# First attention of a hybrid block on one core: another order of work within a group, ScalarE reading two more kinds of banks

## The chip, the cores and the metric

The kernel runs on one core of a Trainium2 chip. The core has five engines that run side by side, each with its own queue of instructions in a fixed order: TensorE (PE; its weight loads are listed as PEld), VectorE (DVE), ScalarE (ACT), GpSimd (POOL) and SyncE (SP, which only issues transfers here). An instruction that waits for another engine waits at the head of its queue, and everything behind it waits too. Products leave TensorE through PSUM, of which this kernel uses eight banks of 128 x 512 float32; ScalarE or VectorE must read a bank before it is given to another product.

The metric is the time of one execution in microseconds (us). Three runs of the kernel before took 2679.74, 2689.66 and 2694.45 us.

## The reference

The input is 16 sequences of 512 tokens with 256 features, all float32: 8192 tokens. Four layers follow each other, each with a residual sum:

```python
x = x + attn_a(layernorm(x))     # softmax attention, 16 heads of 16, rotary
x = x + ffn(layernorm(x))        # 64 routed experts, top 8, and a shared expert
x = x + attn_b(layernorm(x))     # linear attention with a forget gate
x = x + ffn(layernorm(x))

def attn_a(x):
    q, k, v = rope(proj(x, Wq)), rope(proj(x, Wk)), proj(x, Wv)
    attn = softmax(q @ k.T / 4)
    return (attn @ v) @ Wo.T

def ffn(x):
    probs = softmax(x @ router_w.T)
    w, ids = top_k(probs, 8); w = w / sum(w)
    ...
    gu = x @ ws_gate_up
    return routed + (silu(gu[:, :192]) * gu[:, 192:]) @ ws_down
```

The change lies in the first attention, with the part of the first `ffn` that needs no experts: its layernorm, the router and the shared expert.

## The kernel before, in words

A block is 512 tokens, one sequence; there are 16 blocks. Each block has four groups of four heads, and each group four steps, one for each 128 rows of keys or queries. A block is thus 16 steps, numbered 0 to 15 here; step 0 is the first step of group 0, step 4 of group 1, and so on. The order of all instructions of TensorE, VectorE, ScalarE and SyncE is written out by hand: `each(s)` yields the work of step `s`, and what is yielded first is issued first on every engine. GpSimd's order is left to the framework.

What every step does (function `each`, L451): `weighted` computes four score products of the current group `n` (L329, lhsT and rhs with 17 rows of the array for each head, the four heads side by side in the array), and ScalarE takes the exponential of each of the four banks (L369). `largest` computes four score products of group `n + 2` transposed (L329 with 16 rows), and VectorE takes the negated maximum of each bank (L343); the maxima later become a 17th row of the queries, so that the exponentials don't overflow.

What a group does once, with `n` its number:

- `summed(n - 1)` in its first step: 16 products of exponentials and values (L379) into one bank; ScalarE copies the bank (`heads_turned`, L144).
- `turn` of the keys of group `n + 3` in its first step, of the queries in its second: four transposes (L318) into one bank, copied by ScalarE (L323).
- `heads(n - 1)` in its second step (`heads_out`, L147): four transposes (L152) into one bank; VectorE takes the reciprocal of the sums (L156) and multiplies (L160), both reading the bank.
- `row(n + 1)` in its second step: one transpose of the maxima (L351), copied by ScalarE (L359), and four small transfers issued by SyncE that put it into the queries' 17th row.

What a block does once is in two tables, `dense` and `routed`, by step; `(work, far, ...)` means work for block `b + far`. The dense table loads and normalises the tokens two blocks ahead (`load`, `moments`, `normed`, `features`), projects queries and keys (`queries`, L255, with the rotation on GpSimd) and values (`values`, L299), and for the block behind joins the heads (`joined`, L225) and projects the output (`output`, L402; VectorE adds the bank to the residual, L409). The routed table does for the block behind the layernorm, transposes and router of the first `ffn` (`part.moments`, `normed`, `features` L1516, `logits` L1525, `likely`, `exps`), and for two blocks behind the choice of experts (`choose`), the counts (`count` L1582, `added` L1590 for three behind) and the shared expert (`shared`, with its products `gu` L1605 and its `silu` L991 to L993, and `down` L1636). Part of the shared expert of the last three blocks is done after the attention.

All products of this stage take their bank from one pool of eight, `bank()`, in program order and in rotation: the product that takes allocation number `k` waits until allocation `k - 8` has been read. A step takes eight banks for its scores, and one for each further product (`shared` with piece 0 takes two, `features` and `joined` two).

The functions that the diff touches are `heads_out`, `attention` with the inner `heads`, `output` and `each`, and the class `Part` of the `ffn` with `gu`, `silu` and `shared`.

Of the kernel before, what the change touches and what calls it, by code (L numbers as in the profile page):

```python
# [9 lines left out]
F32 = mybir.dt.float32  # L10
U32 = mybir.dt.uint32
AF = mybir.ActivationFunctionType
ALU = mybir.AluOpType
# [4 lines left out]
P = 128  # L18
D = 256
KD = D // P  # L20
H = 16
HD = D // H
HP = 32
NHG = 4
BLK = 512
# [12 lines left out]
class Block:  # L38
# [105 lines left out]
        self.nc.scalar.copy(oT, pav)  # L144
        return oT

    def heads_out(self, out, oT, hg, bank, den_eps=None):  # L147

        nc = self.nc
        pt = bank()  # L150
        for c in range(CB):
            nc.tensor.transpose(pt[:, ts(c, P)], oT[:, ts(c, P)], self.ident)  # L152
        o = pt.rearrange("p (c j k) -> p c j k", j=NHG, k=HP)
        rec = self.small.tile([P, CB, NHG], F32, name="rec")
        if den_eps is None:
            nc.vector.reciprocal(rec, o[:, :, :, HD])  # L156
        else:
            nc.vector.tensor_scalar(rec, o[:, :, :, HD], den_eps, None, ALU.add)
            nc.vector.reciprocal(rec, rec)
        nc.vector.tensor_tensor(  # L160
            out[:, :, ts(hg, NHG * HD)].rearrange("p c (j d) -> p c j d", d=HD),
            o[:, :, :, 0:HD],
            rec.unsqueeze(3).to_broadcast([P, CB, NHG, HD]),
            ALU.mult,
        )


    def attention(self, x, x1, wqkv, wo, rope, part, later):

# [9 lines left out]
        nc, tc = self.nc, self.tc  # L179
        with ExitStack() as c:  # L180
# [6 lines left out]
            p2 = c.enter_context(tc.tile_pool(name="a_2", bufs=2, side="left"))  # L187
# [200 lines left out]
            def heads(n):  # L388
                b, hg = divmod(n, NHG)
                if hg == 0:  # L390
                    aos[b] = p1.tile([P, CB, D], F32, name="ao")
                self.heads_out(aos[b], oTs.pop(n), hg, bank)


            def joined(b):
# [2 lines left out]
            def output(b, i):  # L398
                po = bank()
                for k in range(2):  # L400
                    for kd in range(KD):
                        nc.tensor.matmul(  # L402
                            po[:, ts(k, D)],
                            lhsT=aoTs[b][:, kd, ts(i + k, P)],
                            rhs=wo_sb[:, kd, :],
                            start=(kd == 0),
                            stop=(kd == KD - 1),
                        )
                nc.vector.tensor_tensor(  # L409
                    xs[b][:, i : i + 2, :],  # L410
                    xs[b][:, i : i + 2, :],
                    po.rearrange("p (c d) -> p c d", c=2),
                    ALU.add,
                )
# [6 lines left out]


            dense = {
                0: [(load, 2)],
                2: [(queries, 1, 2)],
                3: [(part.shared, -2, 1), (queries, 1, 3)],
                4: [(joined, -1)],
                6: [(values, 1, 0)],
                7: [(values, 1, 2)],
                8: [(moments, 2)],  # L430
                9: [(normed, 2)],
                10: [(output, -1, 0)],
                11: [(output, -1, 2)],
                13: [(features, 2)],
                14: [(queries, 2, 0)],
                15: [(queries, 2, 1)],
            }
            routed = {
                0: [(part.added, -3)],
                1: [(part.shared, -2, 0)],  # L440
                4: [(part.choose, -2, 0), (part.choose, -2, 1)],
                5: [(part.down, -2, 0), (part.choose, -2, 2)],
                9: [(part.down, -2, 2)],
                12: [(lambda b: part.moments(b, xs[b]), -1)],
                13: [(part.count, -2), (lambda b: part.normed(b, xs.pop(b)), -1)],
                14: [(part.features, -1)],
                15: [(part.logits, -1), (part.likely, -1), (part.exps, -1)],
            }
            steps, groups, z = NHG * CB, self.nblk * NHG, self.nblk - 1

            def each(s):  # L451

                n, i = divmod(s, CB)
                yield groups, n, weighted, i
                yield groups, n + 2, largest, i
                if i == 0:
                    yield groups, n - 1, summed
                    yield groups, n + 3, turn, kTs, H, "kT"
                if i == 1:
                    yield groups, n - 1, heads  # L460
                    yield groups, n + 1, row
                    yield groups, n + 3, turn, qTs, 0, "qT"
                b, at = divmod(s, steps)
                for work, far, *args in dense.get(at, []) + routed.get(at, []):

                    if b + far < z - 2 or work not in (part.shared, part.down):
                        yield self.nblk, b + far, work, *args

            with tc.manual_schedule(
                engines={  # L470
# [517 lines left out]
    def silu(self, out, gate, up, th, half):  # L988

        nc = self.nc  # L990
        nc.scalar.activation(th, gate, AF.Tanh, scale=0.5)  # L991
        nc.vector.scalar_tensor_tensor(th, th, 1.0, gate, ALU.add, ALU.mult)
        nc.vector.scalar_tensor_tensor(out, th, half, up, ALU.mult, ALU.mult)  # L993
# [380 lines left out]
class Part:  # L1374
# [6 lines left out]
    def __init__(self, ctx, k, x, y, weights, room, pairs, side):  # L1381
        rw, self.w_gate, self.w_up, self.w_down, ws_gu, ws_down = weights
        self.ctx, self.pairs, self.slot, self.ws = ctx, pairs, [], {}
        self.k, self.nc, self.x, self.y, self.room = k, k.nc, x, y, room
        tc, T = k.tc, k.T
        self.own = ctx.enter_context(ExitStack())
        self.pools = {
            n: self.own.enter_context(tc.tile_pool(name=f"r_{n}", bufs=n, side=side))
            for n in sorted({1, *room.values()})
        }  # L1390
        self.rows = k.dram.tile([T + P, ROW], F32, name="rows")
        self.counts = k.dram.tile([E, k.nch, P], F32, name="counts")
        (
            self.mvs,
            self.xns,
            self.xnTs,
            self.lgs,
            self.prs,
            self.tops,
            self.rests,  # L1400
            self.chosens,
            self.csums,
            self.hTs,
            self.ys,
            self.gus,
        ) = [{} for _ in range(12)]
        self.end = 0.0
        self.bank = None
        self.shared_weights = (rw, ws_gu, ws_down)
# [187 lines left out]


    def gu(self, b, piece):
        nc, xnT = self.nc, self.xnTs[b]  # L1600
        gu = self.gus[b, piece] = {}
        for m in ((0, 2), (1,))[piece]:
            gu[m] = self.bank()
            for kd in range(KD):
                nc.tensor.matmul(  # L1605
                    gu[m],
                    lhsT=self.wsg_sb[:, kd, ts(m, P)],
                    rhs=xnT[:, kd, :],
                    start=(kd == 0),
                    stop=(kd == KD - 1),  # L1610
                )
        if piece == 1:
            del self.xnTs[b]

    def silu(self, b, piece):
        if piece == 0:
            self.hTs[b] = self.hidden[b % len(self.hidden)]
        gu = self.gus.pop((b, piece))
        high = (P, FT)[piece]
        gate = gu[piece][0:high]  # L1620
        up = gu[2] if piece == 0 else gu[1][FT:P]
        th = self.tile("th", [P, BLK])[0:high]
        self.k.silu(self.hTs[b][0:high, piece, :], gate, up, th, 0.5)

    def shared(self, b, piece):
        self.gu(b, piece)
        self.silu(b, piece)
# [137 lines left out]
```

## Time and profile before

The profiled execution took 2689.83 us; its span, from the first to the last instruction, is 2688.0 us. The stages by time from the span's start, with the busy time of each engine:

| stretch, us | what runs | length | PE | DVE | ACT | POOL | clock |
|---|---|---|---|---|---|---|---|
| 62.20 to 224.46 | first attention, blocks 0 and 1 | 162.26 | 162.26 | 101.97 | 98.02 | 43.25 | 0.97 |
| 224.46 to 1227.69 | first attention, twelve full blocks | 1003.23 | 1003.23 | 695.44 | 599.18 | 235.79 | 1.00 |
| 1227.69 to 1372.70 | first attention, its last blocks | 145.01 | 144.78 | 82.97 | 82.11 | 15.33 | 0.91 |
| 1372.70 to 1700.00 | first experts | 327.30 | 251.62 | 194.72 | 94.56 | 188.97 | 0.90 |
| 1700.00 to 2160.00 | second attention | 460.00 | 442.79 | 438.31 | 262.83 | 119.95 | 1.00 |
| 2160.00 to 2688.00 | second experts | 528.00 | 400.81 | 343.11 | 143.67 | 223.29 | 0.89 |

The costliest rows of the twelve full blocks are the maxima (L343, 683 ns each on VectorE), the exponentials (L369, 602 ns each on ScalarE), the score products (L329) and the sums (L379).

How to read such a table: busy time says how much an engine did, not whether it set the pace. Matmuls are pipelined and a "busy" TensorE may be waiting between two records that overlap in the trace; the chain of waits, which goes back from the last instruction to what released it, and the timeline, which gives start and length of each run of instructions, tell that. The clock is the share of full TensorE clock that was granted.

### The profile page before, as it was taken

What the parts mean: (1) busy time and instruction counts of PE and PEld (TensorE: products, weight loads), DVE (VectorE), ACT (ScalarE), POOL (GpSimd) and SP (SyncE); (2) the same over time, 40 slices, a digit from 0 to 9 for tenths busy, and PEclk for the clock granted to TensorE, in tenths of its full rate; (3) what the DMA queues carried; (4) which work ended last, traced back from release to release, by engine and by line L of the source; (5) the groups of instructions that cost most, each with busy time, mean ns of one, the idle gap of its engine ahead of it and who ended that gap; (6) DMA issues with size and microseconds to landing.
All of it is one profiled execution on the core that took longest, in us unless ns stands there. A gap on an engine that the chain in (4) does not pass through costs nothing.

```text
span 2688.0 us, 47635 instructions
## 1 busy us (share of the span) xinstructions
PE 2447.6 (91%) x17864; PEld 1511.5 (56%) x17864; DVE 1895.4 (71%) x4646; ACT 1291.3 (48%) x2654; POOL 844.7 (31%) x804
## 2 busy tenths in 40 slices
PE   7999999999999999999988885899999969998781
PEld 3445455545455544555446775567667656667671
DVE  6666667666677666776646664899999869967650
ACT  1656556565566655665532332455555523323330
POOL 3122222122221222212015775332232122127773
PEclk7999999999999999999898998999999969999996
DMA  1000111001110001100158986201111058739987
GB/s 57 2 17 19 35 37 35 21 22 35 35 35 21 29 29 35 36 19 21 40 133 234 239 223 145 69 29 60 56 52 53 21 145 184 176 106 262 239 217 147
DMA packets 210003, 226.48 MB, mean 84 GB/s; under 512 B 34286, under 2 KB 202222, under 8 KB 208750
## 3 DMA queue, kind: packets, MB, share of 16 engines
q1 hardware_dynamic: 180366, 174.43, 22.5%
q0 software_dynamic: 25728, 46.15, 8.9%
q8 instruction: 143, 2.34, 0.4%
q10 hardware_dynamic: 3680, 2.85, 0.3%
q14 instruction: 86, 0.70, 0.1%
HBM read 146.50 MB, written 84.48 MB: 86 GB/s over the span
## 4 chain that ended last, share of the span: by engine, by line
PE 68%; DVE 15%; DMA 9%; issue 3%; POOL 1%; ACT 1%; SPq 0%; ACTq 0%; POOLq 0%; DVEq 0%
PE sc L329 20%; PE sc L379 9%; DMA xe<-rows,token 6%; PE sc L255 4%; DVE pT L841 4%; PE sc L1605 3%; PE sc L318 3%; DVE qkT L805 2%; PE sc L299 2%; PE sc L402 2%; PE sc L1636 2%; PE pb L792 2%; PE pb L717 2%; PE sc L1137 2%; PE sc L824 1%
## 5 line engine op out<-in xcount | busy, mean ns | idle before, releaser
L343 DVE TENSOR_REDUCE mx<-sc 128x1 f32<-128x512 f32 x1024 | 635.2, 682 | 375.7 <-PE sc L329 375.6
L369 ACT ACTIVATE pT<-sc 128x512 f32<-128x512 f32 x1024 | 528.6, 602 | 179.5 <-PE sc L329 179.5
L329 PE MATMUL sc<-qT,kT 17*128 17x512 f32 x2048 | 315.6, 646 | 0.0
L329 PE MATMUL sc<-kT,qT 16*128 16x512 f32 x2048 | 312.4, 609 | 1.5 <-DVE mx L343 1.4
L104 POOL TENSOR_SCALAR va<-mv 128x4 f32<-128x4 f32 x64 | 14.7, 230 | 797.1 <-DVE mv L98 797.1
L379 PE MATMUL sc<-pT,v 128*32 128x512 f32 x2048 | 241.8, 614 | 0.0
L329 PEld LDWEIGHTS sc<-kT,qT 16*128 16x128 f32 x2048 | 159.6, 189 | 94.4 <-issue 52.1
L841 DVE SCALAR_TENSOR_TENSOR pT<-sc,of,left 128x256 f32<-128x256 f32 x512 | 204.6, 472 | 4.3 <-PE sc L824 4.3
L277 POOL TENSOR_TENSOR t<-qk,rope_sb 128x512 f32<-128x512 f32 x62 | 78.8, 1270 | 403.4 <-ACT qk L263 396.6
L1107 POOL DMA_INDIRECT xe<-rows,token x128 | 128.5, 1004 | 96.2 <-DVE token L1089 39.0
L379 PEld LDWEIGHTS sc<-pT,v 128*32 128x32 f32 x2048 | 61.3, 112 | 173.1 <-issue 123.0
L329 PEld LDWEIGHTS sc<-qT,kT 17*128 17x128 f32 x2048 | 93.8, 184 | 89.9 <-issue 46.1
L255 PE MATMUL sc<-wqkv_sb,feat 128*128 128x512 f32 x256 | 127.4, 623 | 0.0
L144 ACT COPY oT<-sc 128x512 f32<-128x512 f32 x64 | 37.6, 587 | 169.4 <-PE sc L379 169.4
L792 PE MATMUL pb<-feat,wqk_sb 128*128 128x512 f32 x256 | 117.7, 593 | 0.0
L1172 POOL DMA_INDIRECT routed<-ye,token x64 | 105.0, 1641 | 39.1 <-DMA routed<-ye,token 16.2
L96 DVE BATCH_NORM_STATS2 bn<-x 128x6 f32<-128x256 f32 x256 | 89.0, 410 | 17.7 <-DMA x<-out 12.9
L318 PEld LDWEIGHTS sc<-ident,pad 128*128 128x128 f32 x512 | 54.8, 142 | 74.1 <-issue 38.9
L805 DVE SCALAR_TENSOR_TENSOR qkT<-ez,rz 128x512 f32<-128x512 f32 x64 | 93.9, 1487 | 0.0
L318 PE MATMUL sc<-ident,pad 128*128 128x128 f32 x512 | 86.1, 291 | 5.2 <-POOL pad L293 3.0
L285 POOL TENSOR_TENSOR t<-qk,rope_sb 128x256 f32<-128x256 f32 x124 | 90.7, 753 | 0.0
L1605 PE MATMUL sc<-xnT,wsg_sb 128*128 128x512 f32 x192 | 89.3, 603 | 0.0
(218 smaller groups left out, 4807.0 us busy)
## 6 DMA issues: line engine op xcount, KB each, us to landing
ws<-in_w_gate SPq DMA_DIRECT2D x64, 384.0 KB
ws<-in_w_up SPq DMA_DIRECT2D x64, 384.0 KB
rows<-xn SPq DMA_DIRECT2D x32, 512.0 KB
routed<-y SPq DMA_DIRECT2D x32, 512.0 KB
ws<-in_w_down SPq DMA_DIRECT2D x64, 256.0 KB
x<-in_x SPq DMA_DIRECT2D x16, 512.0 KB
attended<-x SPq DMA_DIRECT2D x16, 512.0 KB
ws<-in_w_down SPq DMA_DIRECT2D x64, 128.0 KB
```

What stands on the lines that cost most here:

```text
L255: nc.tensor.matmul(pq, lhsT=xnTs[b][:, kd, ts(i, P)], rhs=wqkv_sb[:, kd, 0 : 2 * D], start=(kd == 0), stop=(kd == KD - 1),)
L318: nc.tensor.transpose(pt[:, ts(i, P)], pads[b % 2][i][:, at : at + 4, :].rearrange("p h d -> p (h d)"), self.ident,)
L329: nc.tensor.matmul(scs[j], lhsT=lhs[at : at + high, ts(i, P)], rhs=rhs[at : at + high, :], start=True, stop=True,)
L343: nc.vector.tensor_reduce(mxs[n][:, j, i : i + 1], sc, AX.X, ALU.max, negate=True)
L369: nc.scalar.activation(pT[:, j, :], sc, AF.Exp, scale=float(HD) ** -0.5)
L379: nc.tensor.matmul(pav[ts(j, HP), :], lhsT=vs[b % 2][:, i, 4 * hg + j, :], rhs=pT[:, j, :], start=(i == 0), stop=(i == CB - 1),)
L792: nc.tensor.matmul(pq, lhsT=wqk_sb[:, kd, ts(m, P)], rhs=xnTs[b][:, kd, :], start=(kd == 0), stop=(kd == KD - 1),)
L805: nc.vector.scalar_tensor_tensor(qks[b][:, m, :], ez, 1.0, rz, ALU.min, ALU.add)
L841: nc.vector.scalar_tensor_tensor(pTs[n][:, :, ts(s8, HD)], sc[:, :, ts(s8, HD)], of[:, s8 : s8 + 1], here, ALU.mult, ALU.mult,)
L1107: nc.gpsimd.indirect_dma_start(out=xes[e], out_offset=None, in_=rows, in_offset=bass.IndirectOffsetOnAxis(ap=token[:, e : e + 1], axis=0),)
L1172: nc.gpsimd.indirect_dma_start(out=accs[e % 2], out_offset=bass.IndirectOffsetOnAxis(ap=token[:, e : e + 1], axis=0), in_=ye, in_offset=No ...
L1605: nc.tensor.matmul(gu[m], lhsT=self.wsg_sb[:, kd, ts(m, P)], rhs=xnT[:, kd, :], start=(kd == 0), stop=(kd == KD - 1),)
```

## The change

In the first attention:

- A group's first step has only the scores and the sums (`summed`). The turn of the keys moves to the second step, that of the queries to the third.
- In the second step the first entry of the table comes between the keys' turn and the heads.
- The heads' transposes and the output's product are first copied out of PSUM to a new tile `there` by ScalarE; VectorE then works from the copy.
- Both tables become one, and entries move: `count` from step 13 to 10, `joined` from 4 to 5, the second `values` from 7 to 9, `features` from 13 to 11, `queries` of two blocks ahead from 14 and 15 to 13 and 15, the router's transposes (`part.features`) from 14 to 15, `choose` piece 2 from 5 to 6, `down` from 5 and 9 to 7 and 14.
- The first piece of the shared expert, which took two banks at once in step 1, is split into `gate` (step 1) and `up` (step 3); the second piece moves from step 3 to step 5.

```diff
-    def heads_out(self, out, oT, hg, bank, den_eps=None):
+    def heads_out(self, out, oT, hg, bank, pool, den_eps=None):
 ...
-        o = pt.rearrange("p (c j k) -> p c j k", j=NHG, k=HP)
+        there = pool.tile([P, BLK], F32, name="there")
+        nc.scalar.copy(there, pt)
+        o = there.rearrange("p (c j k) -> p c j k", j=NHG, k=HP)
 ...
-                self.heads_out(aos[b], oTs.pop(n), hg, bank)
+                self.heads_out(aos[b], oTs.pop(n), hg, bank, p2)
 ...
+                there = p2.tile([P, BLK], F32, name="there")
+                nc.scalar.copy(there, po)
                 nc.vector.tensor_tensor(
                     xs[b][:, i : i + 2, :],
                     xs[b][:, i : i + 2, :],
-                    po.rearrange("p (c d) -> p c d", c=2),
+                    there.rearrange("p (c d) -> p c d", c=2),
                     ALU.add,
                 )
 ...
             dense = {
-                0: [(load, 2)],
+                0: [(load, 2), (part.added, -3)],
+                1: [(part.gate, -2)],
                 2: [(queries, 1, 2)],
-                3: [(part.shared, -2, 1), (queries, 1, 3)],
-                4: [(joined, -1)],
-                6: [(values, 1, 0)],
-                7: [(values, 1, 2)],
+                3: [(part.up, -2), (queries, 1, 3)],
+                4: [(part.choose, -2, 0), (part.choose, -2, 1)],
+                5: [(part.shared, -2, 1), (joined, -1)],
+                6: [(values, 1, 0), (part.choose, -2, 2)],
+                7: [(part.down, -2, 0)],
                 8: [(moments, 2)],
-                9: [(normed, 2)],
-                10: [(output, -1, 0)],
-                11: [(output, -1, 2)],
-                13: [(features, 2)],
-                14: [(queries, 2, 0)],
-                15: [(queries, 2, 1)],
+                9: [(values, 1, 2), (normed, 2)],
+                10: [(output, -1, 0), (part.count, -2)],
+                11: [(features, 2), (output, -1, 2)],
+                12: [(lambda b: part.moments(b, xs[b]), -1)],
+                13: [(queries, 2, 0), (lambda b: part.normed(b, xs.pop(b)), -1)],
+                14: [(part.down, -2, 2)],
+                15: [
+                    (part.features, -1),
+                    (queries, 2, 1),
+                    (part.logits, -1),
+                    (part.likely, -1),
+                    (part.exps, -1),
+                ],
             }
-            routed = {
 ...
-            }
+            expert = part.gate, part.up, part.shared, part.down
 ...
+                b, at = divmod(s, steps)
+                now = [
+                    (self.nblk, b + far, work, *args)
+                    for work, far, *args in dense[at]
+                    if b + far < z - 2 or work not in expert
+                ]
                 if i == 0:
                     yield groups, n - 1, summed
+                if i == 1:
                     yield groups, n + 3, turn, kTs, H, "kT"
-                if i == 1:
+                    yield from now[0:1]
                     yield groups, n - 1, heads
                     yield groups, n + 1, row
+                    now = now[1:]
+                if i == 2:
                     yield groups, n + 3, turn, qTs, 0, "qT"
 ...
+                yield from now
 ...
+    def gate(self, b):
+        gu = self.bank()
+        self.chunk(b, 0, gu)
+        self.hTs[b] = self.hidden[b % len(self.hidden)]
+        th = self.ths[b] = self.tile("th", [P, BLK])
+        self.nc.scalar.activation(th, gu, AF.Tanh, scale=0.5)
+        self.nc.vector.scalar_tensor_tensor(th, th, 1.0, gu, ALU.add, ALU.mult)
+
+    def up(self, b):
+        gu = self.bank()
+        self.chunk(b, 2, gu)
+        self.nc.vector.scalar_tensor_tensor(
+            self.hTs[b][:, 0, :], self.ths.pop(b), 0.5, gu, ALU.mult, ALU.mult
+        )
```

`chunk(b, m, to)` is the product of one third of the shared weights, two matmuls, that `gu` did before in a loop of its own.

More of the change, by code (lines that the diff above doesn't have):

```diff
@@ L423, in attention @@
             dense = {
-                0: [(load, 2)],
+                0: [(load, 2), (part.added, -3)],
+                1: [(part.gate, -2)],
                 2: [(queries, 1, 2)],
-                3: [(part.shared, -2, 1), (queries, 1, 3)],
-                4: [(joined, -1)],
-                6: [(values, 1, 0)],
-                7: [(values, 1, 2)],
-                8: [(moments, 2)],
-                9: [(normed, 2)],
-                10: [(output, -1, 0)],
-                11: [(output, -1, 2)],
-                13: [(features, 2)],
-                14: [(queries, 2, 0)],
-                15: [(queries, 2, 1)],
-            }
-            routed = {
[L439 to L447, printed above, removed]
-            }
+                3: [(part.up, -2), (queries, 1, 3)],
[3 more added lines that the diff above has]
+                7: [(part.down, -2, 0)],
+                8: [(moments, 2)],
+                9: [(values, 1, 2), (normed, 2)],
[11 more added lines that the diff above has]
+                ],
+            }
+            expert = part.gate, part.up, part.shared, part.down
             steps, groups, z = NHG * CB, self.nblk * NHG, self.nblk - 1
@@ L455, in each @@
                 yield groups, n + 2, largest, i
+                b, at = divmod(s, steps)
[4 more added lines that the diff above has]
+                ]
                 if i == 0:
                     yield groups, n - 1, summed
+                if i == 1:
                     yield groups, n + 3, turn, kTs, H, "kT"
-                if i == 1:
+                    yield from now[0:1]
                     yield groups, n - 1, heads
                     yield groups, n + 1, row
+                    now = now[1:]
+                if i == 2:
                     yield groups, n + 3, turn, qTs, 0, "qT"
[L463 to L467, printed above, removed]
+                yield from now
             with tc.manual_schedule(
@@ L1405, in __init__ @@
             self.gus,
-        ) = [{} for _ in range(12)]
+            self.ths,
+        ) = [{} for _ in range(13)]
         self.end = 0.0
@@ L1599, in gu @@
     def gu(self, b, piece):
-        nc, xnT = self.nc, self.xnTs[b]
         gu = self.gus[b, piece] = {}
@@ L1603, in gu, with chunk @@
             gu[m] = self.bank()
[L1604 to L1611, printed above, removed]
+            self.chunk(b, m, gu[m])
         if piece == 1:
             del self.xnTs[b]
+    def chunk(self, b, m, to):
+        for kd in range(KD):
+            self.nc.tensor.matmul(
+                to,
+                lhsT=self.wsg_sb[:, kd, ts(m, P)],
+                rhs=self.xnTs[b][:, kd, :],
+                start=(kd == 0),
+                stop=(kd == KD - 1),
+            )
     def silu(self, b, piece):
@@ L1623, in silu @@
         self.k.silu(self.hTs[b][0:high, piece, :], gate, up, th, 0.5)
+    def gate(self, b):
[10 more added lines that the diff above has]
+            self.hTs[b][:, 0, :], self.ths.pop(b), 0.5, gu, ALU.mult, ALU.mult
+        )
     def shared(self, b, piece):
```

## The prediction

> **What bounds the kernel now.** I read the windows first, then the chain of waits, then the timeline of a block. The windows give the first attention's steady part, twelve blocks from 224 to 1228 us (columns: length, then busy time of PE, weight loads, DVE, ACT and POOL, clock, DMA):
>
> ```profile
> 224.46:1227.69 1003.23, 1003.23 (x6721) 507.72 (x6721) 695.44 (x1549) 599.18 (x1176) 235.79 (x264) 1.00 0.10 29
> ```
>
> TensorE is busy for all of it at full clock; VectorE has 31% and ScalarE 40% left. The chain (start, length, what) stays on TensorE there, and shows what its time is made of:
>
> ```profile
> 475.27 3.48 PE sc L1605 x8
> ...
> 558.88 3.48 PE sc L1605 x8
> ...
> 602.98 1.93 PE sc L329 x16
> 604.91 1.92 PE sc L402 x8
> 606.84 2.35 PE sc L329 x15
> ...
> 621.93 2.42 PE sc L329 x15
> 627.14 1.96 PE sc L329 x16
> 632.74 2.16 PE sc L329 x16
> ```
>
> The same line returns after 83.61 us: that is a block of 16 steps. A step's scores for exponentials and maxima (L329, eight banks) take 1.93 us undisturbed. Four steps of the block take more: 2.35 (step 11), 2.42 (14), 1.96 (15), 2.16 (step 0 of the next block). The excess, 0.42 + 0.49 + 0.03 + 0.23 = 1.17 us, is all that TensorE waits in a block. The rest, 82.4 us, is streaming and the gaps between products of different shape.
>
> Who makes it wait is in the timeline. Allocation n of the eight banks waits until allocation n-8 has been read, so the first four extra products of a step take the banks of the exponentials, the next those of the maxima, and what is left last falls on the next step's scores. Step 10 ends in one extra product, the output (L402); its bank is the eighth of step 11:
>
> ```profile
> 607.33 0.68 DVE L409 TENSOR_TENSOR x<-x,sc 128x512 f32<-128x512 f32 x1
> 607.73 1.46 PE L329 MATMUL sc<-kT,qT 16*128 16x512 f32 x8
> ```
>
> DVE adds only behind its four maxima (2.48 us), until 608.01; the eight records from 607.73 take 1.46 instead of 1.04. A release that is 0.3 late costs 0.42 (in step 14 the heads' bank, 0.43 late, costs 0.49): lateness plus 0.06 to 0.1.
>
> **The change, part by part.** Times below count from the first score of a step, as at 597.71: maxima's scores at 0.97, next product at 1.93, exponentials from 1.16 to 3.22 (598.87 + 2.07), maxima on DVE 2.02 to 4.50 (599.73 + 2.48). A freed bank reaches TensorE 0.05 later (a feat copy ends at 1376.19, its product starts at 1376.24).
>
> *Shapes.* Gaps stand only where the shape changes: 0.10 at the first record, and 0.06 (transposes) or 0.10 (512 or 256 columns) at the second. A group has eleven such changes now: L329 to 379 to 318 to 329; 329 to 152 to 351 to 318 to 329; and in two more steps 329 to a dense product and back. With the k turn behind the next step's scores and the q turn one step later it has nine: 329 to 379 to 329; 329 to 318 (the dense product and the heads' transposes follow without a gap, as 1605 now follows 318) to 351 to 329; two more steps as before. L379 straight to L329 is in the trace where no turns are left: 3.57 for the sums at 1357.13, as with the turn behind it. So 2 x 4 x 0.16 = 1.28 us saved in a block; a turn instead of a 512-column product first behind the scores saves 0.05 in each group, 0.19; step 5's joined transposes now stand behind the row product, -0.16; features lead steps 11 and 15, 0.10. Sum: 1.41 us.
>
> *Old waits.* The output's and the heads' banks go to ScalarE, which has read them about 0.6 us after the product; the count and features leave step 13. The waits of steps 11, 14 and 15 go: 0.94. The 0.23 of step 0 stays: its bank is the logits', last of step 15 as before, and DVE still reads it twice.
>
> *ScalarE.* Four heads and two outputs of 0.58 us (the other attention has this copy, 577 ns) are 3.5 us more in a block for ScalarE, 60% to 64% busy. They lie under TensorE's 1.7 us products. Without that cover each would delay the next bank.
>
> *VectorE's own time* does not fall. Reading PSUM or a copy is one price here:
>
> ```profile
> L884 DVE TENSOR_TENSOR ao<-there,rec 128x256 f32<-128x256 f32 x64 | 27.2, 425 | 2.2
> L160 DVE TENSOR_TENSOR ao<-sc,rec 128x256 f32<-128x256 f32 x64 | 27.1, 424 | 2.2
> L913 DVE TENSOR_TENSOR x<-x,added 128x512 f32<-128x512 f32 x32 | 21.8, 682 | 5.6 <-ACT added L910 5.6
> L409 DVE TENSOR_TENSOR x<-x,sc 128x512 f32<-128x512 f32 x32 | 21.6, 676 | 6.2 <-PE sc L402 6.2
> ```
>
> [...]
>
> *A new wait on VectorE.* In steps 9 and 13 VectorE's queue holds maxima, heads, then the normalisation. Now the heads start right behind the maxima:
>
> ```profile
> 602.41 0.42 DVE L160 TENSOR_TENSOR ao<-sc,rec 128x256 f32<-128x256 f32 x1
> 603.34 1.38 DVE L122 TENSOR_SCALAR tok<-x,mv,rstd 128x256 f32<-128x256 f32 x4
> 604.93 2.48 DVE L343 TENSOR_REDUCE mx<-sc 128x1 f32<-128x512 f32 x4 [0.21 <-PE sc L329]
> ```
>
> After it they wait for ScalarE's copy. The heads' transposes stand behind k turn and dense product (1.93 + 0.49 + 1.72), end at 4.57 and can be copied from 4.77; ScalarE starts at 4.9 and ends at 5.5. VectorE idles 4.5 to 5.52, divides and multiplies until 6.2, normalises until 8.05. Steps 9 and 13 last 4.99, so in steps 10 and 14 the maxima start at 3.05 instead of 2.02, and free their banks at 3.8, 4.4, 5.0 and 5.6. Step 10 (three extras) lasts 4.68, and the fourth score of step 11 needs the third maximum: 0.30 late, cost 0.38. Step 14 (two extras) lasts 4.24; step 15's sixth score, due at 5.21, needs the fourth: 0.39 late, cost 0.45. Bounds: 0 where ScalarE copies the heads ahead, 1.0 each where the whole shift reaches TensorE.
>
> *Another, in step 5.* The second shared piece, heads, row and two joined products make 14 banks, and the shared one falls on step 6's fourth score. Its chain now:
>
> ```profile
> 737.29 0.59 ACT L991 ACTIVATE th<-sc 64x512 f32<-64x512 f32 x1 [0.73 <-PE sc L1605]
> 737.91 0.68 DVE L992 SCALAR_TENSOR_TENSOR th<-th,sc 64x512 f32<-64x512 f32 x1
> 738.62 0.69 DVE L993 SCALAR_TENSOR_TENSOR hT<-th,sc 64x512 f32<-64x512 f32 x1
> ```
>
> tanh starts 1.96 after the product, here at 2.42 + 1.96 = 4.38, and the last product ends 2.02 later, at 6.40; step 6 starts at 6.02. 0.42 late, cost 0.46. Bounds 0 and 0.8.
>
> *Gate and up apart* cost nothing: gate's bank is free at 5.75 and is asked for at 5.96 by step 2's sixth score, up's at 5.3 against 6.5. Moved work keeps its cover: the counts' transposes, the features and the second shared output meet buffers whose readers ended at least two steps before; on SP the store of y is issued at step 14 instead of 9, ahead of only the next load, which is needed eight steps later; GpSimd rotates the last queries of a block two steps apart instead of one (4.2 us each: 1.27 + 1.44 + 1.27 and gaps), and the k turn that reads them comes a step later. At the stage's end GpSimd's last routing product stands behind four memsets now (1.91 us at 1396.81); its first reader, a gather, starts at 1418.97. In the tail the heads and first output gain a copy each on the way to the end: +1.3 us.
>
> *Sum.* Saved 1.41 + 0.94, new 0.38 + 0.45 + 0.46 = 1.29: 1.06 us a block, 12.7 for twelve. Blocks 0, 1 and 15 lack part of the work and are held by VectorE and ScalarE; I take them as even, block 14 at -1.0, the tail at +1.3. Total 12.4. The profiled execution took 2689.83 us (span 2688.0), the median of the runs 2689.66 within 2679.74 to 2694.45: 2677 us.
>
> **Rivals.** *Nothing new waits* (28%): if a late release is absorbed because the other three rows of the array go on, the 1.29 fall away: 2.35 x 12 = 28 us, 2662. For it: in step 14 three products do go on while the fourth waits (three records start at 622.83, one at 622.90). Against: 0.43 late costs 0.49 in step 14.
> *The gaps are not the shapes'* (9%): a record behind a gap mostly waits for a bank too, and if that is the gap it only moves. Then 0.94 - 1.29 = -0.35, 4 us more: 2694. Against: L1605 at 725.92 waits for a bank as well and follows L318 with no gap.
> *ScalarE's queue becomes the bound* (14%, slower): in steps 0, 4, 8, 12 (oT) and 1, 9, 13 (the row's mT, now behind the heads' copy) the eighth score of the next step waits for ScalarE's last copy, by my count with 0.18 to spare. ScalarE does fall behind: the qk copy at 631.10 waited 0.81 for GpSimd. From 0.33 late seven waits of 0.15 eat the gain; 0.45 late costs 7 x 0.35 = 2.45, 1.4 x 12 = 17 us: 2707. Against: oT is read within 0.8 of the sums now, and queries are spread out.
>
> **How the numbers follow.** Forecast 47%, 2677 (2668 to 2686 alone); 2% for anything else. A measurement tells 0.5%, 13.4 us, from no change, so the line is 2676.2: half of the forecast and all of the first rival lie below, 0.53; the other half and the second rival within, 0.32; the rest 0.15. The range, 2655 to 2697, holds the forecast and the first two rivals with the spread of the runs shown.
>
> **What would show it.** The block's period, now 83.61, should be 82.5; sums followed at once by L329; scores of 1.93 everywhere but steps 6, 11 and 15 (2.3 to 2.4) and 0 (2.16); maxima of steps 10 and 14 starting 1 us later. A period above 83.6, or scores of over 2 us behind the sums, would make it wrong.

## The result, and the profile after

The changed kernel takes 2729.06 us in the median of four runs (2726.93 to 2732.77), the kernel before 2686.07 (four runs, 2679.74 to 2694.45). The ratio is 1.0161, 95% interval 1.0142 to 1.018: slower by 1.6%, and 32 us above the upper end of my range. The profiled execution took 2727.29 us, its span is 2725.2. Most line numbers of the first attention are 5 higher than before (scores L329 are now L334, sums L379 are L384); the heads' copy is L154, the heads' product L162 (before L160), the output's copy L415.

The windows of the changed kernel, twelve blocks from the first score of one to the first score of another (span, then busy time of TensorE, weight loads, VectorE, ScalarE, GpSimd, then granted clock, DMA share, GB/s):

```profile
224.77:1259.70 1034.93, 1026.86 (x6722) 525.35 (x6721) 724.15 (x1547) 635.50 (x1248) 238.10 (x265) 0.98 0.09 28
```

Twelve blocks took 1003.23 us before and take 1034.93, 86.24 each instead of 83.61; I had forecast 82.5. TensorE is no longer busy all the time, and its clock is no longer full. The first fifteen steps of a block sum to 75.0 us, as my forecast has it within 0.7. The whole miss stands in step 15: its length is 10.8 us in nine of the twelve blocks and 12.45 in the other three, 11.2 in the mean, instead of some 6.8.

The chain of waits of the changed kernel through steps 13, 14 and 15 (start, length, what):

```profile
551.70 0.59 PE sc L323 x4
552.28 1.73 PE sc L260 x4
...
554.60 0.58 ACT there L154
...
555.20 0.27 DVE rec L158
...
555.49 0.82 DVE ao L162
556.31 0.63 DVE t L113
...
556.96 0.68 DVE t L114
...
557.66 0.17 DVE rstd L116
...
557.86 2.22 DVE xn L122 x4
560.09 0.61 DVE mx L348
...
560.74 2.93 PE sc L334 x12
563.67 1.62 PE sc L1529 x8
565.29 2.81 PE sc L260 x4
```

Before, the chain stayed on TensorE here. Now it leaves TensorE for VectorE: the heads, then the normalisation of step 13, and only behind them the first maximum of step 14, which frees the bank that step 15's third score waits for. That order I had foreseen. The lengths I had not: the two small steps of the normalisation took 152 and 162 ns before, its four pieces 1.38 us, the heads' product 0.42. The sum of these excesses is 2.3 us. VectorE's timeline at this place in the kernel before, where the same normalisation took 1.96 us in all (start, length, instruction):

```profile
622.17 0.15 DVE L113 SCALAR_TENSOR_TENSOR t<-y 128x4 f32<-128x4 f32 x1
622.36 0.16 DVE L114 TENSOR_TENSOR t<-t,va 128x4 f32<-128x4 f32 x1
...
622.75 1.38 DVE L122 TENSOR_SCALAR xn<-x,mv,rstd 128x256 f32<-128x256 f32 x4
```

The groups of VectorE's instructions over the same twelve blocks of the changed kernel (count, busy time in us, mean ns of one, idle before):

```profile
L122 DVE TENSOR_SCALAR xn<-x,mv,rstd 128x256 f32<-128x256 f32 x48 | 26.7, 616 | 0.4
L162 DVE TENSOR_TENSOR ao<-there,rec 128x256 f32<-128x256 f32 x48 | 25.1, 523 | 2.5
L122 DVE TENSOR_SCALAR tok<-x,mv,rstd 128x256 f32<-128x256 f32 x48 | 16.6, 411 | 0.4
L113 DVE SCALAR_TENSOR_TENSOR t<-y 128x4 f32<-128x4 f32 x24 | 10.2, 426 | 0.0
L114 DVE TENSOR_TENSOR t<-t,va 128x4 f32<-128x4 f32 x24 | 10.0, 415 | 0.8
```

The same instruction on the same shape takes 411 ns in step 9 (tok) and 616 in step 13 (xn). So it is not the code but the place. What else is at this place shows in GpSimd's timeline of the changed kernel (start, length, instruction, idle time before and what ended it):

```profile
554.76 1.27 POOL L282 TENSOR_TENSOR t<-qk,rope_sb 128x512 f32<-128x512 f32 x1 [3.03 <-ACT qk L268]
555.98 1.63 POOL L290 TENSOR_TENSOR t<-qk,rope_sb 128x256 f32<-128x256 f32 x2
557.69 1.28 POOL L298 TENSOR_TENSOR pad<-t,t 128x512 f32<-128x512 f32 x1
```

This is the rotation of the queries that the change moves from step 14 to step 13. It runs from 554.76 to 558.97, exactly beside the normalisation, and the ends agree: the product L162, which needs 0.42 alone, ends 0.28 us after L282; L113 and L114 each end 0.02 us after a GpSimd instruction (556.93 after 556.91, 557.63 after 557.61); the first piece of L122 ends 0.15 after L298. Before, GpSimd was idle from 618.6 to 627.0, and the normalisation ran from 622.17 to 624.13. The end of that idle time in GpSimd's timeline of the kernel before:

```profile
627.02 1.27 POOL L277 TENSOR_TENSOR t<-qk,rope_sb 128x512 f32<-128x512 f32 x1 [8.45 <-ACT qk L263]
```

The second loss is the clock. Windows of the changed kernel, one of the rest of step 13 with step 14, one of the part of step 15 behind its scores (the clock is the third number from the end):

```profile
551.62:558.94 7.32, 7.32 (x47) 4.34 (x43) 6.09 (x10) 5.53 (x12) 4.21 (x5) 1.00 0.00 1
...
563.60:569.75 6.15, 6.15 (x31) 4.44 (x28) 1.98 (x4) 1.76 (x3) 0.84 (x1) 0.72 0.39 116
```

From 564.50 to 566.50 the granted clock is 0.50, and 0.72 over 6.15 us is 3.4 us at 0.50. Such a stretch comes in each of the twelve blocks, behind the wait; in three of them it lasts twice as long, 6.8 us.

### The profile page after: what moved, and what is told of

Its sections match the earlier page's. It is cut to its first block, busy times and chain, and to the rows that moved or that the text cites. A ratio compares the mean times of both kernels' runs of the same rounds, so it can differ in the third digit from the quotient of the medians.

```text
span 2725.2 us, 47672 instructions
## 1 busy us (share of the span) xinstructions
PE 2483.4 (91%) x17864; PEld 1537.9 (56%) x17864; DVE 1929.5 (71%) x4646; ACT 1337.0 (49%) x2750; POOL 847.1 (31%) x804
## 4 chain that ended last, share of the span: by engine, by line
PE 66%; DVE 17%; DMA 9%; issue 3%; ACT 2%; POOL 2%; SPq 0%; ACTq 0%; POOLq 0%; DVEq 0%
PE sc L334 19%; PE sc L384 9%; PE sc L260 5%; DMA xe<-rows,token 5%; DVE pT L853 4%; PE sc L1623 3%; PE sc L323 3%; DVE qkT L817 2%; PE sc L1149 2%; PE sc L407 2%; PE sc L304 2%; PE pb L804 2%; PE pb L729 2%; DVE xn L122 2%; PE pb L1149 1%
## 5 line engine op out<-in xcount | busy, mean ns | idle before, releaser
L334 PE MATMUL sc<-qT,kT 17*128 17x512 f32 x2048 | 333.7, 644 | 9.7 <-DVE mx L348 9.7
L334 PE MATMUL sc<-kT,qT 16*128 16x512 f32 x2048 | 308.5, 612 | 0.3 <-DVE mx L348 0.3
L384 PE MATMUL sc<-pT,v 128*32 128x512 f32 x2048 | 246.3, 624 | 0.0
L282 POOL TENSOR_TENSOR t<-qk,rope_sb 128x512 f32<-128x512 f32 x62 | 78.7, 1270 | 438.3 <-ACT qk L268 431.6
L334 PEld LDWEIGHTS sc<-kT,qT 16*128 16x128 f32 x2048 | 151.1, 188 | 90.4 <-issue 32.9
L334 PEld LDWEIGHTS sc<-qT,kT 17*128 17x128 f32 x2048 | 100.0, 183 | 146.0 <-issue 99.2
L384 PEld LDWEIGHTS sc<-pT,v 128*32 128x32 f32 x2048 | 62.2, 114 | 175.6 <-issue 125.7
L260 PE MATMUL sc<-wqkv_sb,feat 128*128 128x512 f32 x256 | 137.7, 667 | 0.0
L1583 POOL TENSOR_TENSOR wt<-pr,chosen 128x256 f32<-128x256 f32 x32 | 23.3, 729 | 243.4 <-DVE chosen L1578 217.3
L290 POOL TENSOR_TENSOR t<-qk,rope_sb 128x256 f32<-128x256 f32 x124 | 93.2, 773 | 0.0
```

The costliest lines, as they stand in the source:

```text
L260: nc.tensor.matmul(pq, lhsT=xnTs[b][:, kd, ts(i, P)], rhs=wqkv_sb[:, kd, 0 : 2 * D], start=(kd == 0), stop=(kd == KD - 1),)
L290: eng.tensor_tensor(t2[:, :, lo : lo + HD // 2], qk2[:, :, :, 1 - half], rope_sb[:, i, HD + lo : HD + lo + HD // 2] .unsqueeze(1) .to_broa ...
L334: nc.tensor.matmul(scs[j], lhsT=lhs[at : at + high, ts(i, P)], rhs=rhs[at : at + high, :], start=True, stop=True,)
L384: nc.tensor.matmul(pav[ts(j, HP), :], lhsT=vs[b % 2][:, i, 4 * hg + j, :], rhs=pT[:, j, :], start=(i == 0), stop=(i == CB - 1),)
```

## The experiments

Each was timed beside the kernel before, which had a median of 2686.74 us in the first four, 2688.47 in the next four and 2688.34 in the last. Two theories stood against each other: that GpSimd's rotation beside the normalisation slows VectorE, and that the heads' detour through ScalarE alone makes the maxima late.

**The rotation back in step 14** (below: the exchanged version). The second shared output takes its place in step 13:

```diff
-                13: [(queries, 2, 0), (lambda b: part.normed(b, xs.pop(b)), -1)],
-                14: [(part.down, -2, 2)],
+                13: [(part.down, -2, 2), (lambda b: part.normed(b, xs.pop(b)), -1)],
+                14: [(queries, 2, 0)],
```

> The changed kernel with two entries of its table exchanged: the queries of block b+2 go back from step 13 to step 14, the second shared output goes from step 14 to step 13. Theory GpSimd: in step 13 the rotation on GpSimd (four products of 0.74 to 1.28 us) runs beside VectorE's normalisation, and each VectorE instruction that reads SBUF ends only when the running GpSimd instruction does; that is the 2.26 us by which the maxima of step 14 start later than I predicted. Then here the normalisation's instructions fall from 616 to 408 ns on average, the scores of step 15 from about 4.9 us to 2.0-2.4, the clock stays at full speed in the steady part, a block takes 81.6 to 82.4 us instead of 86.3, and the time is 2662 to 2682 us. Theory copy: the wait comes from the heads' detour through ScalarE alone, and the rotation is innocent; then nothing changes: scores of step 15 at 4.7 to 5.5 us, 2720 to 2735 us. If the low clock comes from denser work and not from the wait, the windows at half clock remain while the scores get short, and a block takes 83 to 85 us.

Measured: 2674.65 us (8 runs, 2669.03 to 2683.85), ratio to before 0.9962 (0.9941 to 0.9982). VectorE's timeline in step 13 of this kernel, then the start of the rotation in GpSimd's, the scores of step 15 in the chain, and the windows over twelve blocks:

```profile
618.79 0.25 DVE L158 RECIPROCAL rec<-there 128x16 f32<-128x16 f32 x1 [0.96 <-ACT there L154]
619.08 0.42 DVE L162 TENSOR_TENSOR ao<-there,rec 128x256 f32<-128x256 f32 x1
619.42 0.15 DVE L113 SCALAR_TENSOR_TENSOR t<-y 128x4 f32<-128x4 f32 x1
...
620.00 1.38 DVE L122 TENSOR_SCALAR xn<-x,mv,rstd 128x256 f32<-128x256 f32 x4
621.30 2.47 DVE L348 TENSOR_REDUCE mx<-sc 128x1 f32<-128x512 f32 x4
```

```profile
623.40 1.27 POOL L282 TENSOR_TENSOR t<-qk,rope_sb 128x512 f32<-128x512 f32 x1 [8.04 <-ACT qk L268]
```

```profile
622.64 2.32 PE sc L334 x16
```

```profile
220.23:1202.10 981.87, 981.87 (x6721) 505.24 (x6720) 695.43 (x1547) 630.39 (x1248) 235.77 (x265) 1.00 0.10 30
```

Every duration of the normalisation and the heads' product is back at what it was, the wait of 0.96 us for the copy is still there, the scores of step 15 take 2.32 us, the clock is full, a block takes 81.82. Two lines of a table are worth 54 us. The copy theory, which saw no difference coming, falls.

**The copy taken away, the rotation left in step 13.**

```diff
-        there = pool.tile([P, BLK], F32, name="there")
-        nc.scalar.copy(there, pt)
-        o = there.rearrange("p (c j k) -> p c j k", j=NHG, k=HP)
+        o = pt.rearrange("p (c j k) -> p c j k", j=NHG, k=HP)
```

> The changed kernel with the heads read by VectorE straight from PSUM again (no copy by ScalarE in front of the reciprocal); everything else as changed, the rotation still in step 13. Theory GpSimd: the reciprocal and the product move some 0.5 us ahead, the normalisation still meets the rotation; its first three or four instructions stay at 0.6 to 1.3 us each, the scores of step 15 still take 3.3 to 4.7 us and the time is 2705 to 2735 us. Theory copy: the normalisation ends about 1 us after the maxima as before the change, the scores of step 15 take 1.9 to 2.4 us and the time falls to 2665 to 2690 us.

Measured: 2732.04 us (4 runs), ratio 1.017 (1.0139 to 1.0202). VectorE's timeline in step 13 of this kernel; the rotation runs from 557.06 to 561.09:

```profile
557.08 0.42 DVE L160 TENSOR_TENSOR ao<-sc,rec 128x256 f32<-128x256 f32 x1
557.42 0.93 DVE L113 SCALAR_TENSOR_TENSOR t<-y 128x4 f32<-128x4 f32 x1
558.38 0.67 DVE L114 TENSOR_TENSOR t<-t,va 128x4 f32<-128x4 f32 x1
559.08 0.67 DVE L116 SCALAR_TENSOR_TENSOR rstd<-t,y 128x4 f32<-128x4 f32 x1
559.78 2.42 DVE L122 TENSOR_SCALAR xn<-x,mv,rstd 128x256 f32<-128x256 f32 x4
```

The normalisation starts earlier and ends hardly earlier: it walks in GpSimd's step, one instruction per GpSimd instruction (L113 ends at 558.35 and L116 at 559.75, each 0.02 us behind a GpSimd instruction). Only the heads' product, which now reads one operand from PSUM, keeps 0.42 us beside the rotation. The scores of step 15 take 4.4 to 5.4 us, and a block is 0.85 longer than in the changed kernel: without the copy steps 2 and 6 are 0.49 and 0.31 longer.

**GpSimd work alone, in the kernel before.** Four products of 128x512 in GpSimd's idle stretch of step 13, which nothing reads:

```diff
+            def idle_turns(n):
+                qT = qTs[n]
+                for k in range(4):
+                    t = f1.tile([P, BLK], F32, name="t3")
+                    nc.gpsimd.tensor_tensor(t, qT, qT, ALU.mult)
...
+                if at == 13 and b >= 0:
+                    yield groups, n + 3, idle_turns
```

> The kernel before with nothing changed but four more GpSimd products (128x512, 1.27 us each by the rotation's rows) in step 13 of each block, started by the q copy at 621.24 in the block of the profile; GpSimd is idle there (618.6 to 627.0), nothing reads what they write. Theory GpSimd: VectorE's instructions on SBUF operands in step 13 (113, 114, 116 and the first 122) wait for these products, the maxima of step 14 start 2.0 to 3.5 us later, the scores of step 15 take 2.8 to 4.3 us instead of 1.96, and the time is 2697 to 2725 us, more where the clock falls too. Theory copy: GpSimd work in an idle stretch costs nothing: 2683 to 2690 us, and the normalisation's instructions keep 408 ns on average.

Measured: 2710.57 us, ratio 1.0096 (1.0066 to 1.0126). VectorE and GpSimd in step 13 of this kernel, each from its own timeline, then the scores of step 15 in the chain:

```profile
628.87 0.42 DVE L160 TENSOR_TENSOR ao<-sc,rec 128x256 f32<-128x256 f32 x1
...
629.46 0.16 DVE L114 TENSOR_TENSOR t<-t,va 128x4 f32<-128x4 f32 x1
629.65 0.89 DVE L116 SCALAR_TENSOR_TENSOR rstd<-t,y 128x4 f32<-128x4 f32 x1
630.58 2.98 DVE L122 TENSOR_SCALAR xn<-x,mv,rstd 128x256 f32<-128x256 f32 x4
```

```profile
628.37 4.40 POOL L329 TENSOR_TENSOR t<-qT 128x512 f32<-128x512 f32 x4 [2.76 <-ACT qT L323]
```

```profile
634.38 3.01 PE sc L335 x15
```

The effect without the change: L116 takes 0.89 us instead of 0.16, the four pieces 2.98 instead of 1.38. Not all instructions wait: L114 started in the 0.08 us between the first two of the four products. The scores of step 15 take 3.01 us in every block. And the clock fell in only four of thirteen blocks; two windows of step 15 in this kernel, one of each kind:

```profile
549.45:556.11 6.66, 6.66 (x38) 4.00 (x37) 4.13 (x7) 3.40 (x7) 4.52 (x5) 1.00 0.53 161
634.31:642.66 8.35, 8.35 (x38) 4.60 (x37) 4.12 (x7) 3.39 (x7) 4.52 (x5) 0.80 0.41 126
```

The same work and the same wait, 1.7 us apart at a clock of 1.00 and of 0.80: that is the price of one stretch of low clock by itself.

**Fills in place of products.** The same stretch, with instructions that write and do not read:

```diff
-                for k in range(4):
-                    t = f1.tile([P, BLK], F32, name="t3")
-                    nc.gpsimd.tensor_tensor(t, qT, qT, ALU.mult)
+                t = f1.tile([P, BLK], F32, name="t3")
+                nc.gpsimd.tensor_tensor(t[:, 0:4], qT[:, 0:4], qT[:, 0:4], ALU.mult)
+                for k in range(8):
+                    nc.gpsimd.memset(t, 0.0)
```

> The kernel before with the same GpSimd stretch in step 13 filled by instructions that only write: one product of 128x4 that starts with the q copy, then eight fills of 128x512 (64x512 takes 526 ns in the profile of before, so some 4.2 us in all, as long as the four products of the run with 1.04 us each). Theory 'any running GpSimd instruction holds up VectorE': instructions 113, 114, 116 and the first of 122 each wait for the end of a fill, up to 0.5 us each, 1.0 to 2.0 us in all, the scores of step 15 take 2.2 to 3.0 us, and the time is 2692 to 2708 us. Theory 'only GpSimd's reading of SBUF does, for VectorE instructions with two SBUF operands': 113, 114 and 116 keep 150 to 165 ns; the time stays at 2683 to 2692 us, or a little above where 122, with one tensor operand, still waits.

Measured: 2692.32 us, ratio 1.0022 (1.0005 to 1.004). The fills run from 621.44 to 626.15; VectorE beside them, then the scores of step 15 in the chain:

```profile
622.03 0.15 DVE L113 SCALAR_TENSOR_TENSOR t<-y 128x4 f32<-128x4 f32 x1
622.22 0.16 DVE L114 TENSOR_TENSOR t<-t,va 128x4 f32<-128x4 f32 x1
622.41 0.16 DVE L116 SCALAR_TENSOR_TENSOR rstd<-t,y 128x4 f32<-128x4 f32 x1
622.61 2.49 DVE L122 TENSOR_SCALAR xn<-x,mv,rstd 128x256 f32<-128x256 f32 x4
```

```profile
627.00 1.95 PE sc L336 x16
```

The three instructions with two operands from SBUF do not notice the fills; L122, with one large operand, takes 0.62 us a piece instead of 0.35. A block stays at 83.61: the maxima are 1.1 us late, and step 15 has that much room in the kernel before. The 4 us in the median fit the last blocks: in the single profiled executions one of them takes 83.06 instead of 80.40 and the next 72.20 instead of 70.38, 4.5 us together.

**The other side moved: normalisation in step 14, rotation left in step 13.**

```diff
-                13: [(queries, 2, 0), (lambda b: part.normed(b, xs.pop(b)), -1)],
-                14: [(part.down, -2, 2)],
+                13: [(queries, 2, 0)],
+                14: [(part.down, -2, 2), (lambda b: part.normed(b, xs.pop(b)), -1)],
```

> The changed kernel with the normalisation of block b-1 moved from step 13 to step 14, behind that step's maxima; the rotation of the queries stays in step 13. Theory GpSimd: the rotation runs from 5.1 to 9.3 us after step 13's start, the normalisation now from 9.5, so only the heads' product still waits for it (819 ns instead of 424 in one of four); the normalisation's instructions keep 408 ns on average, scores of step 15 take 1.9 to 2.1 us, the router's transposes wait some 0.3 us for the later result, the clock stays full, a block takes 81.5 to 82.0 us, and the time is 2668 to 2682 us. If the slow instructions belonged to the copy or to the step and not to the rotation beside them, they would stay slow in step 14 and the time above 2690 us.

Measured: 2666.17 us, ratio 0.992 (0.9897 to 0.9943), a block 81.46, both a little under what I expected. xn is back at 409 ns a piece; the heads' product, still beside the rotation, at 522 in the mean and 0.82 in step 13. Either of the two may move, as long as they part; with the normalisation moved step 15's wait of 0.39 us goes as well (scores 1.93). The 0.3 us that I expected the router's transposes to wait did not appear.

**Normalisation in front of the heads.** From the exchanged version:

```diff
-                    yield from now[0:1]
+                    first = 2 if at in (9, 13) else 1
+                    yield from now[0:first]
                     yield groups, n - 1, heads
                     yield groups, n + 1, row
-                    now = now[1:]
+                    now = now[first:]
```

> The exchanged version (queries in step 14, second shared output in 13) with the normalisations of steps 9 and 13 put in front of the heads on VectorE. My prediction's step 'a new wait on VectorE': VectorE idles about 1 us for the heads' copy and the normalisation behind it delays the next maxima; in the exchanged version that cost 0.17 us in step 11 and 0.39 in step 15. If so, both go: scores of steps 11 and 15 at 1.93 us, a block at 81.2 to 81.4 us instead of 81.83, 6 to 8 us less than the exchanged version in all: 2664 to 2671 us. If the two waits have another origin: no difference, 2670 to 2680 us.

Measured: 2658.93 us (2657.27 to 2660.92), ratio 0.9903 (0.9885 to 0.9921). The scores of steps 11 and 15 take 1.93 us, a block 81.32: the 0.17 and 0.39 us were VectorE's idling for the copy. The median fell further than the 6 us of the blocks, by 15.7, and below the expected range; the single profiled execution has 6.4 of it ahead of the first block's logits.

**Logits ahead of the queries.** On top of that, to free the bank of step 0 earlier:

```diff
-                14: [(queries, 2, 0)],
-                15: [
-                    (part.features, -1),
-                    (queries, 2, 1),
-                    (part.logits, -1),
+                14: [(part.features, -1), (queries, 2, 0)],
+                15: [
+                    (part.logits, -1),
+                    (queries, 2, 1),
```

> As the version with the normalisations in front, and the router's transposes of xn in step 14, its logits ahead of the queries in step 15, so that the bank that step 0's eighth score takes is read by ScalarE (queries) and not twice by VectorE (logits). By the bank rule of the prediction the 0.23 us in step 0 goes, and one change of shape: 0.2 to 0.4 us a block, a block at 80.8 to 81.1 us, 2658 to 2668 us. Against it: the logits could wait for ScalarE's copies of the transposes, or VectorE's readings of the logits could meet the rotation of the queries of step 14; then a block takes 81.3 us or more.

Measured: 2653.67 us (2643.12 to 2658.44), ratio 0.9879 (0.9858 to 0.9901), the lowest median of all: 1.2% faster than the kernel before, 2.8% faster than the changed one. Step 0's scores take 1.93 us, so its wait is gone. But a block takes 81.25, only 0.07 less, and not the 0.2 to 0.4 expected: steps 14 and 15 together became 0.15 longer. The saved change of shape did not come.

**The order of the sums alone, in the kernel before.**

```diff
                     yield groups, n - 1, summed
-                    yield groups, n + 3, turn, kTs, H, "kT"
                 if i == 1:
+                    yield groups, n + 3, turn, kTs, H, "kT"
                     yield groups, n - 1, heads
                     yield groups, n + 1, row
+                if i == 2:
                     yield groups, n + 3, turn, qTs, 0, "qT"
```

> The kernel before with the order of the sums alone: the k turn goes from behind the sums to the head of the group's second step, the q turn to its third step; no copies by ScalarE, gate and up together, table as before. My prediction's step 'shapes': two shape changes fewer per group, 1.28 us a block, and no new wait, 12 to 15 blocks: 2664 to 2674 us. Rival of the prediction (the gaps are not the shapes'): 2680 to 2692 us.

Measured: 2677.76 us, ratio 0.9967 (0.9948 to 0.9987), a block 82.57. Right in sign, too small in size: the block loses 1.04 us, but 0.51 of it are waits (step 14's goes; step 11's only moves to step 12), 0.53 the shapes. Whether the rest of the 1.28 needs the other rows of the table, which put transposes beside transposes, no run shows.

**The copies alone, in the kernel before** (the heads' copy as in the change, and the output's).

```diff
+                there = p2.tile([P, BLK], F32, name="there")
+                nc.scalar.copy(there, po)
...
-                    po.rearrange("p (c d) -> p c d", c=2),
+                    there.rearrange("p (c d) -> p c d", c=2),
```

> The kernel before with the copies alone: heads and outputs out of PSUM by ScalarE, order and table as before. My prediction's step 'old waits': the waits of steps 11, 14 and 15 (0.42, 0.49 and 0.03 us) go, the 0.23 of step 0 stays, no new wait as the heads' transposes come first behind the scores here and the copy ends before the maxima do; a block takes 82.6 to 82.8 us instead of 83.61, and the time is 2671 to 2680 us. Rival: ScalarE's longer queue delays other banks by as much: 2683 to 2695 us.

Measured: 2679.18 us, ratio 0.997 (0.9956 to 0.9984), a block 82.84. Step 11's wait goes, step 14 keeps 0.14 of its 0.49: 0.77 us of the 0.94.

The versions side by side; a block is the mean distance of the logits over the steady part:

| version | block, us | scores of step 15, us | median, us |
|---|---|---|---|
| before | 83.61 | 1.96 | 2686 to 2688 |
| changed | 86.24 | 4.7 to 5.5 | 2729.06 |
| changed, heads from PSUM | 87.1 | 4.4 to 5.4 | 2732.04 |
| before, GpSimd products | 85.4 | 3.01 | 2710.57 |
| before, GpSimd fills | 83.61 | 1.95 | 2692.32 |
| rotation in step 14 | 81.82 | 2.32 | 2674.65 |
| normalisation in step 14 | 81.46 | 1.93 | 2666.17 |
| and in front of the heads | 81.32 | 1.93 | 2658.93 |
| and logits first | 81.25 | 1.93 | 2653.67 |

## Why the prediction was wrong, point by point

**The step that failed** stands in the paragraph on gate and up: "Moved work keeps its cover", and there "GpSimd rotates the last queries of a block two steps apart instead of one (4.2 us each ...)". I had asked who waits for GpSimd and how long its queue is, and never beside which VectorE instructions the rotation would now run. The three runs that put the two together lose (1.016, 1.017, 1.0096), the runs that part them gain. From it follows the number "normalises until 8.05": the maxima of step 14 were to start 3.05 us into the step, and start 5.31 into it (560.00 against 554.69). With the rotation back in step 14 they start 2.96 into it.

**The price of a late bank** was off too. I had counted lateness plus 0.06 to 0.1. In the changed kernel the late bank makes the scores of step 15 2.7 to 3.5 us longer (4.66 to 5.50 instead of 1.96), and behind them come 3.4 to 6.8 us at a clock of 0.50, that is 1.7 to 3.4 us more. Both together make step 15 4.4 us longer than in the exchanged version (11.2 in the mean against 6.8), and 12 times 4.4 is 53 of the 54 us between the two medians.

**None of my rivals was it.** The slower one, ScalarE's queue, did not come: step 0 keeps its 2.16 us and the other steps behind sums and rows 1.93.

**"Reading PSUM or a copy is one price"** holds where VectorE is alone (425 ns in the exchanged version, 424 before) and fails beside GpSimd: 0.82 us from the copy, 0.42 from PSUM, in the same place.

**Shapes, 1.41 us a block**: right in size, not shown in its make-up. In the exchanged version a block is 1.79 shorter than before; its waits went from 1.17 to 0.17 + 0.39 + 0.23 = 0.79, so 1.41 are left for the shapes. That is a remainder, and the order of the sums, to which I gave 1.28, brought 0.53 by itself; no run shows what brings the rest.

**New waits**: step 15 0.39 (forecast 0.45), step 11 0.17 (0.38). VectorE finished the maxima of step 10 a little sooner than I had added up: they started 2.97 us into the step, not 3.05, and take 1.88, not 1.95, to the third. That their origin is VectorE's wait for the copy is shown by the run with the normalisation in front. **Step 6, 0.46**: nothing. The chain of the shared piece ran as I had it (tanh 4.34 us after the step's start, the last product's end at 6.37), but the fourth score of step 6 started with the others, 0.33 before that end: the bank was another one. My rule of n-8 does not give the right slot here; why the pool hands it out differently I did not trace.

**The sum.** Without the collision the forecast of 2677 would have met the exchanged version's 2674.65, partly by luck. In the single profiled executions twelve blocks gave 21.4 us (forecast 12.7). The start, up to the first logits, took 5.6 us longer (I had put the first blocks down as even), and the last blocks, up to the last sum with the residual (L409, now L416), 2.9 longer (forecast 0.3). Both losses stand at a low clock, for which I had no term. The first group of block 0, up to its sums, takes 21.36 us at a mean clock of 0.76; before, it took 16.14 at 1.00. There the turn of the keys no longer parts the scores of steps 0 and 1. From the last score to the last sum with the residual it is 21.19 us at 0.76 instead of 13.36 at 1.00, while the blocks ahead of it are shorter. That the new order lowers the clock at these two places is a reading; no run tests it alone. What follows that sum took 0.7 less, and 1301 to 1310 us in the eleven single executions, so this difference says nothing. In the changed kernel the start cost 10.1 us, some 6 of them in the last group of block 1, which has the collision already; the twelve blocks cost 31.7, the last blocks gave back 1.5, and what follows 3.2.

**What I could have read.** The trace of before holds the collision elsewhere, in the second attention. The summary of L113 in the kernel before (durations in ns: min/median/max), then VectorE's and GpSimd's timeline at one place:

```profile
L113 DVE SCALAR_TENSOR_TENSOR t<-y x64: 150/154/604, 12.4 to 2349.7; 128x4 f32<-128x4 f32 x64
```

```profile
2191.02 0.60 DVE L113 SCALAR_TENSOR_TENSOR t<-y 128x4 f32<-128x4 f32 x1
```

```profile
2190.88 0.72 POOL L1570 TENSOR_TENSOR wt<-pr,chosen 128x256 f32<-128x256 f32 x1 [1.89 <-DVE chosen L1565]
```

An instruction on four columns that takes 604 ns at its worst and 154 otherwise; its end, 2191.62, stands 0.02 behind that of GpSimd's product, 2191.60. I had taken medians and means, and looked at no maximum.

## What to carry to other kernels

When a step of GpSimd is moved, list the VectorE instructions with SBUF operands that will then run beside it and price each at the length of a GpSimd instruction, not at its own (here L113 took 0.93 us where the GpSimd instruction beside it took 1.27, and 0.15 alone). Look for the same instruction with two very different durations in the trace you have: min, median and max of one line show a collision that a mean hides. And where TensorE is the bound, count a wait once for itself and ask what the clock does behind it: here 1.7 to 3.4 us more behind every wait of 2.7 us or more in the changed kernel, 1.7 us more in some of the blocks behind one of 1.05 us, nothing behind 0.39 us.

## What the runs showed of the hardware

In these runs GpSimd holds VectorE up by kind of instruction. Beside GpSimd products, L113, L114 and L116 (two SBUF operands, 0.15 to 0.16 us alone) that are held up end 0.02 us behind the GpSimd instruction and take up to 0.93 us; beside fills they keep 0.15 to 0.16. L122 (one SBUF operand of 256 columns, SBUF result) is held up by both: its four pieces take 1.38 us alone, 2.22 to 2.98 beside products and 2.49 beside fills. The reductions from PSUM (0.67 to 0.69) and the product with one operand in PSUM (0.42) are held up by neither. GpSimd loses too: the pair of products L290 takes 1.63 us beside the heads' product from the copy, and 1.44 where that product reads PSUM. For the heads' product the place of its operand makes the difference, 0.82 us from the copy and 0.42 from PSUM; why fills hold up L122 and not the other three no run shows.

The clock of TensorE fell to 0.50 in the changed kernel, for 3.4 us (0.72 over 6.15 us) or twice that, behind a wait of 2.7 us or more in each of the twelve blocks. In the kernel with the GpSimd products it fell behind a wait of 1.05 us in four blocks of thirteen (0.80 over 8.35 us in one of them), and in the exchanged version behind 0.39 us in none (1.00 over the 6.80 us of one step 15, and over the twelve blocks). What length of wait lowers it no run shows.
